# An edge-gated graph layer on one core: the gated halves made on GpSimd, the add done in place a tile ahead, z made in the rows of h

## The chip, the cores and the metric

The kernel runs on one core of a Trainium2 chip. The metric is the device time of one execution in microseconds. Engines are named as in the profile: PE is TensorE's matmuls, PEld its weight loads, DVE is VectorE, ACT is ScalarE, POOL is GpSimd, SP is SyncE, which here only issues DMAs. Every engine runs its own instructions strictly in the order in which they were written down.

## The reference

There are 16 graphs (`b`) with 1024 nodes and 256 features and one adjacency matrix for all, 1024 x 1024 with few entries that aren't zero. It is given as `A_a` and as `A_m`:

```python
pre_u = jnp.einsum('bud,dk->buk', h_t, W1[:d])
pre_v = jnp.einsum('bvd,dk->bvk', h_t, W1[d:])
hidden = jax.nn.relu(pre_u[:, :, None, :] + pre_v[:, None, :, :] + b1)
S = jax.nn.sigmoid(jnp.einsum('buvk,ko->buvo', hidden, W2)[..., 0] + b2[0])
a_t = jnp.einsum('buv,bud->bvd', S * A_a, h_t)
m_t = jnp.einsum('uv,bud->bvd', A_m, h_t) * h_t
z_t = beta1 * h_t + beta2 * (jnp.einsum('bvd,de->bve', a_t, Wa) + ba) + beta3 * (jnp.einsum('bvd,de->bve', m_t, Wm) + bm)
```

Each node `v` collects its neighbours' rows twice: weighted with the adjacency value (`m`), and with that value times a gate per edge and graph (`a`).

## The kernel before, in words

**Tiling.** Graphs go in four groups of `GB` = 4, nodes `v` in eight tiles of 128. A block is one group and one node tile; there are `BS` = 32 blocks, in the order of `order`. The edges of a node tile are sorted into two halves of 64 nodes (`w`), and each half into `TW` = 5 tiles of 128 edges (`j`). So a block has ten steps `s`, and the program has 320 steps `n`.

**Before the steps** the kernel makes neighbour lists from the adjacency (`lists`, for four of the node tiles up front and for the other four between the steps), and tables in DRAM, one for each group, whose row for a node holds `pre_u` of four graphs and `h` of four graphs: 8 KB. `rows` makes the `pre_u` part on PE (`w_u`, L427) with a copy on ACT (L443) and a store on SP (L446). Tables 1 to 3 are filled between the steps; the calls of `plan` give the steps of each load and of its two pieces.

**A step** `n` has these parts, each a function:

- `fetch` (L496): an indirect DMA on POOL fetches one row of the table for each of the 128 edges into `fetched[n % NF]`, `NF` = 6 places. The fetch for step n+5 is issued in step n, behind the aggregation of n-1, whose place it takes. `fetch_val` (L382) fetches adjacency values in the same queue, two in a step while there are any (80 in all, ten of them ahead of the steps).
- `expand` (L569): two matmuls on PE spread `pre_v + b1` of the 64 nodes to their edges, into the PSUM tile `pc`, of which there are two. It is called for n+2 near the end of step n.
- `left_adj` (L579): ACT writes the adjacency value, one-hot over 16 nodes, into the half of `left` that isn't gated, four times over, once for each graph. `left` has one slot of nodes (64 elements for both kinds and four graphs of 16 nodes: one quarter) or two, by `QUARTERS`: in the five tiles 1, 2, 2, 2, 1.
- `gate` (L601, L606, L609, L612): VectorE adds the fetched `pre_u` and `pc` into the one tile `t` (L601, 128 x 1024); four times, once for each graph, it takes the relu, multiplies by `W2` and sums (L606, with a read of the accumulator); ACT makes the sigmoid (L609) and then writes the gated half of `left` in four operations (L612). `fill` puts a list operation in front of each L606 while lists are made.
- `aggregate` (L623), called for n-1 in step n, ahead of the gate of n: matmuls of `left` with the fetched `h`, 8 or 16 matmul records, into `acc`.

**The end of a block** runs in the next block's steps. `half_end` copies `acc` (L631); `turn_over` transposes it (L641, steps 1, 7, 7, 9) and ACT copies it into `LT` (L644); VectorE multiplies the ungated half by `h` (L654). `block_end` (steps 3 to 6) multiplies with `Wa` and `Wm` (L672) in two halves; ACT copies each half out of PSUM into `z` (L675), VectorE adds `beta1 * h` two steps later (L676), and SP stores `z` (L678). `h` itself is the tile `h_blk`, loaded by SP in step 0 (L775). `halves` (steps 0, 2, 3, 5, 6) makes the next block's `pre_v`: `w_v` on PE (L427, behind a row of bias, L431), ACT copies (L461, L462, L465, L468) and a subtraction on VectorE (L463). All these PSUM tiles, `misc`, come from two banks of `psm`.

**What orders the work.** The order is written out by hand (`manual_schedule`): the order of the calls in the loop from L745 on is the order of each engine's queue. `after(step, f)` puts `f` down for a later step, and `do(step)` runs what is due, behind the gate of that step. SP runs as far ahead as its waits allow.

Of the kernel before, what the change touches and what calls it, by code (L numbers as in the profile page):

```python
# [13 lines left out]
P = 128  # L14
# [3 lines left out]
def kernel(  # L18
# [210 lines left out]
    NF = 6  # L229
# [327 lines left out]

    marks, pcs, accs, evs, hbs, LTs, lefts = {}, {}, {}, {}, {}, {}, {}
# [38 lines left out]

    def gate(n):
        k, g, vt, w, j = where(n)
        t = one.tile([P, GB, D], FP, name="t")  # L600
        nc.vector.tensor_tensor(t, fetched[n % NF][:, :GD].rearrange("p (b d) -> p b d", b=GB),  # L601
                                pcs.pop(n).rearrange("p (b d) -> p b d", b=GB), ALU.add)
# [5 lines left out]
        gt = wk.tile([P, GB], FP, name="gt")  # L608
        nc.scalar.activation(gt, sc, AF.Sigmoid, bias=b2_b)  # L609
        for b in range(GB):  # L610
            m = len(QUARTERS[j])
            nc.scalar.activation(lefts[n][:, :m, b, 1, :], lefts[n][:, :m, b, 0, :], AF.Copy, scale=gt[:, b:b + 1])  # L612

    def aggregate(n):
        k, g, vt, w, j = where(n)
        left, f = lefts.pop(n), fetched[n % NF]
        for i, q in enumerate(QUARTERS[j]):
# [4 lines left out]
            for b in range(GB):  # L622
                nc.tensor.matmul(accs[h][b * 2 * V:(b + 1) * 2 * V, r, :],  # L623
                                 left[:, i, b].rearrange("p k v -> p (k v)"), f[:, GD + b * D:GD + (b + 1) * D],
                                 start=first, stop=(j == q + 1), skip_group_check=True)
# [7 lines left out]
    def turn_over(k, w, q, step):  # L633
        if w == 0 and q == 0:
            LTs[k] = one.tile([P, DC, GB, 2, P], FP, name="LT")
        LT = LTs[k]
        pt = small("pt")
        ev = evs.pop(q)
        for i in range(4):
            r, c = divmod(i, DC)  # L640
            nc.tensor.transpose(pt[:, i * P:(i + 1) * P], ev[:, r, c * P:(c + 1) * P], ident)  # L641
        v = slice(w * W + q * U, w * W + (q + 1) * U)
        r = (w * W + q * U) // V
        nc.scalar.copy(LT.rearrange("p c b k (r v) -> p r (c b k) v", v=V)[:, r:r + 2],  # L644
                       pt.rearrange("p (r i v) -> p r i v", r=2, v=V))
# [6 lines left out]
        def times_h():  # L652
            m = LT[:, :, :, 0, v]
            nc.vector.tensor_tensor(m, m, hTs[order[k]].rearrange("p b c n -> p c b n")[:, :, :, v], ALU.mult)  # L654
# [4 lines left out]
    def block_end(k):  # L659
# [3 lines left out]
        z = big.tile([P, GB, D], FP, name="z", bufs=1)  # L663
        for h in range(2):
            for i, wt in ((1, w_a), (0, w_m)):
# [4 lines left out]
                for bb in range(2):  # L670
                    for c in range(DC):
                        nc.tensor.matmul(pz[:, bb * D:(bb + 1) * D], LTs[k][:, c, 2 * h + bb, i, :], wt[:, c, :],  # L672
                                         start=False, stop=(i == 0 and c == DC - 1), skip_group_check=True)
# [18 lines left out]
    def tail(parts, step):  # L692
# [8 lines left out]
        for i, wt in enumerate((w_m, w_a)):  # L701
            for r in range(len(parts)):
                for d in range(DC):
                    for b in range(c):
                        bb = r * c + b
                        nc.tensor.matmul(pz[b * m:(b + 1) * m, r * D:(r + 1) * D], LT[:, d, bb, i, v:v + m],  # L706
# [19 lines left out]
    def plan(blocks, ns):  # L726

        for k, (load, *pieces) in zip(blocks, ns):
# [7 lines left out]
                                                                             for i in range(2, NT - 1)), (223, 231, 233)))  # L736
# [7 lines left out]
    total = BS * T  # L744
    for n in range(total + 2):  # L745
        k, s = divmod(n, T)
        if 1 <= n <= total:
# [13 lines left out]
        if n + 2 < total:  # L761
            expand(n + 2)
# [181 lines left out]
```

## Time and profile before

| what | value |
|---|---|
| median of 3 runs | 1150.17 us (1149.06 to 1153.97) |
| the profiled execution, first to last instruction | 1165.8 us; the profile gives no time around it |
| busy | PE 94%, DVE 91%, ACT 77%, POOL 38% |
| granted TensorE clock | 0.976 on average, 1.00 from 310 us on |
| DMA | 391.40 MB, mean 336 GB/s |

The profile gives busy time by engine, groups of instructions by line with their mean duration and the idle time ahead of them, and timelines with the start of every instruction in us from the start of the span. Two things help in reading it. A duration on DVE, ACT and PE has a tail in which the next instruction already runs, so what an instruction costs in a full queue is the distance between two starts. And the waiting of an engine is put down to whatever came last, which in a queue can be the instruction ahead of the one that had to wait.

### The profile page before, as it was taken

The numbers are of one execution on the slowest core, as the hardware profiler recorded it, in microseconds if no ns is written. First come the engines' busy times: TensorE is split into PE (matmuls) and PEld (weight loads), VectorE is DVE, ScalarE is ACT, GpSimd is POOL, SyncE is SP. The second block draws the span as 40 slices with busy tenths as digits, with TensorE's granted clock in tenths as the row PEclk, the third lists the DMA queues.
The fourth block names the chain that finished last, engine by engine and source line by source line (L and its number), as shares of the span: only waits on it lengthen the run. The fifth ranks groups of instructions, "written<-read, shape, count | busy, mean of one in ns | idle before, by whom it ended". The sixth has DMA issues, their size and how long they took to land. (4 is left out here: it accounts for less than half of the span.)

```text
span 1165.8 us, 23918 instructions
## 1 busy us (share of the span) xinstructions
PE 1092.1 (94%) x7633; PEld 723.1 (62%) x7633; DVE 1056.2 (91%) x3487; ACT 893.5 (77%) x2624; POOL 439.9 (38%) x428
## 2 busy tenths in 40 slices
PE   7867899999999999999999999999999999999986
PEld 6744666666666666666666666666666666666553
DVE  7688889888999989999999999999999999999994
ACT  2346587767887878888888888888888888888873
POOL 1556645253335333443333333333333333333330
PEclk9868899999999999999999999999999999999999
DMA  9986898999999999999999999999998998999991
GB/s 286 298 307 223 277 372 312 362 320 331 342 320 323 396 379 336 358 350 402 389 374 369 355 364 356 360 364 383 371 375 324 361 322 333 334 339 328 328 346 60
DMA packets 147048, 391.40 MB, mean 336 GB/s; under 512 B 16753, under 2 KB 105329, under 8 KB 110705
## 3 DMA queue, kind: packets, MB, share of 16 engines
q0 software_dynamic: 50016, 300.50, 68.9%
q1 hardware_dynamic: 81616, 74.99, 20.0%
q10 hardware_dynamic: 15280, 14.29, 3.7%
q8 instruction: 63, 1.03, 0.3%
q14 instruction: 73, 0.59, 0.1%
HBM read 393.78 MB, written 50.33 MB: 381 GB/s over the span
## 5 line engine op out<-in xcount | busy, mean ns | idle before, releaser
L496 POOL DMA_INDIRECT fetched<-table,uidx x320 | 341.5, 1067 | 628.3 <-PE acc L623 447.2
L606 DVE SCALAR_TENSOR_TENSOR t<-t,w_b 128x256 f32<-128x256 f32 x1280 | 478.3, 421 | 19.3 <-ACT left L612 0.5
L601 DVE TENSOR_TENSOR t<-fetched,pc 128x1024 f32<-128x1024 f32 x320 | 389.3, 1217 | 41.4 <-PE pc L569 13.9
L623 PE MATMUL acc<-fetched,left 128*32 128x256 f32 x4096 | 336.2, 391 | 31.9 <-ACT left L612 26.2
L612 ACT ACTIVATE left<-left,gt 128x32 f32<-128x32 f32 (+1 forms) x1280 | 299.3, 304 | 10.4
L569 PE MATMUL pc<-X,mark 128*128 128x512 f32 x640 | 237.6, 453 | 6.2 <-ACT mark L562 5.0
L623 PEld LDWEIGHTS acc<-fetched,left 128*32 128x32 f32 x4096 | 130.6, 109 | 179.3 <-issue 52.4
L569 PEld LDWEIGHTS pc<-X,mark 128*128 128x128 f32 x640 | 97.2, 191 | 140.0 <-issue 89.3
L609 ACT ACTIVATE gt<-sc,b_b 128x4 f32<-128x4 f32 x320 | 96.2, 301 | 43.4 <-DVE t L606 40.8
L672 PE MATMUL misc<-w_m,LT 128*128 128x256 f32 x496 | 117.2, 379 | 0.0
L672 PE MATMUL misc<-w_a,LT 128*128 128x256 f32 x496 | 117.1, 379 | 0.0
L579 ACT ACTIVATE left<-onehot,val 128x128 f32<-128x128 bf16 (+1 forms) x320 | 116.5, 364 | 0.0
L427 PE MATMUL misc<-w_v,hT 128*128 128x256 f32 x448 | 107.3, 383 | 0.0
L427 PE MATMUL misc<-w_u,hT 128*128 128x256 f32 x416 | 101.2, 390 | 5.7 <-ACT few L329 3.6
L606 DVE DVE_READ_ACCUMULATOR t<-t,w_b 128x1 f32 x1280 | 104.0, 81 | 0.0
L672 PEld LDWEIGHTS misc<-w_a,LT 128*128 128x128 f32 x496 | 93.9, 189 | 15.1
L672 PEld LDWEIGHTS misc<-w_m,LT 128*128 128x128 f32 x496 | 93.8, 189 | 14.9
L382 POOL DMA_INDIRECT val<-in_adjT_dram,vidx x80 | 85.7, 1071 | 35.1 <-issue 22.4
L427 PEld LDWEIGHTS misc<-w_v,hT 128*128 128x128 f32 x448 | 86.0, 192 | 13.9
L427 PEld LDWEIGHTS misc<-w_u,hT 128*128 128x128 f32 x416 | 79.5, 195 | 17.3 <-ACT few L329 3.7
L631 ACT COPY ev<-acc 128x512 f32<-128x512 f32 x128 | 75.5, 590 | 14.6 <-PE acc L623 4.2
L675 ACT COPY z<-misc 128x512 f32<-128x512 f32 x62 | 36.3, 586 | 58.1 <-PE misc L672 38.8
(164 smaller groups left out, 947.9 us busy)
## 6 DMA issues: line engine op xcount, KB each, us to landing
h_blk<-in_x_dram SPq DMA_DIRECT2D x31, 512.0 KB
out_dram<-z SPq DMA_DIRECT2D x31, 512.0 KB
hT<-in_xT_dram SPq DMA_DIRECT2D x28, 512.0 KB
table<-in_x_dram ACTq DMA_DIRECT2D x24, 512.0 KB
table<-tab SPq DMA_DIRECT2D x24, 512.0 KB
fetched<-table,uidx POOLq DMA_INDIRECT x320
table<-in_x_dram SPq DMA_DIRECT2D x8, 512.0 KB
table<-fetched SPq DMA_DIRECT2D x8, 512.0 KB
```

The costliest lines, as they stand in the source:

```text
L382: nc.gpsimd.indirect_dma_start(out=val[:, i, j:j + 1], out_offset=None, in_=adj_flat, in_offset=bass.IndirectOffsetOnAxis(ap=vidx[:, i, j: ...
L427: nc.tensor.matmul(p[:, bb * D:(bb + 1) * D], hT[:, 2 * h + bb, i, :], wt[:, i, :], start=(i == 0 and not begun), stop=(i == DC - 1), skip ...
L496: nc.gpsimd.indirect_dma_start(out=fetched[n % NF], out_offset=None, in_=table[g], in_offset=bass.IndirectOffsetOnAxis(ap=uidx[:, vt * NW ...
L569: nc.tensor.matmul(pcs[n][:, c], marks[n // TW][:, j * P:(j + 1) * P], cuts[k][:, w, c], start=True, stop=True)
L579: nc.scalar.activation(lefts[n][:, :m, :, 0, :], onehot[:, i, o:o + m, :].unsqueeze(2).to_broadcast([P, m, GB, V]), AF.Copy, scale=val[:, ...
L601: nc.vector.tensor_tensor(t, fetched[n % NF][:, :GD].rearrange("p (b d) -> p b d", b=GB), pcs.pop(n).rearrange("p (b d) -> p b d", b=GB), ...
L606: nc.vector.scalar_tensor_tensor(t[:, b, :], t[:, b, :], 0.0, w2_b, ALU.max, ALU.mult, accum_out=sc[:, b:b + 1])
L609: nc.scalar.activation(gt, sc, AF.Sigmoid, bias=b2_b)
L612: nc.scalar.activation(lefts[n][:, :m, b, 1, :], lefts[n][:, :m, b, 0, :], AF.Copy, scale=gt[:, b:b + 1])
L623: nc.tensor.matmul(accs[h][b * 2 * V:(b + 1) * 2 * V, r, :], left[:, i, b].rearrange("p k v -> p (k v)"), f[:, GD + b * D:GD + (b + 1) * D ...
L631: nc.scalar.copy(evs[q], accs.pop(q))
L672: nc.tensor.matmul(pz[:, bb * D:(bb + 1) * D], LTs[k][:, c, 2 * h + bb, i, :], wt[:, c, :], start=False, stop=(i == 0 and c == DC - 1), sk ...
```

## The change

- `NF` goes from 6 to 7. The fetch for step n+6 is now issued in step n.
- The add is a function of its own, `add`, works in the fetched rows themselves and is called for n+1 in step n, ahead of the gate of n. `add(0)` stands in front of the loop.
- `gate` ends with the sigmoid. `weigh` makes the gated halves of all four graphs in one GpSimd operation, called for n-1 at the start of step n, ahead of the aggregation of n-1 and of the fetch that follows it.
- `left` has two gated slots around one ungated slot that both use, so `left_adj` writes half as much. `LT` is laid out to match: for every second graph the two kinds are swapped, and `turn_over`, `times_h`, `block_end` and `tail` index it so.
- `expand(n + 2)` moves from behind `do(n)` to the start of step n.
- `z` has no tile any more. L675 is gone; VectorE reads PSUM and writes into `h_blk`, one step after the matmuls rather than two, and `h_blk` is what is stored.
- The last table row's steps go from (223, 231, 233) to (222, 230, 232).

```diff
-    NF = 6
+    NF = 7
...
-        lefts[n] = wk.tile([P, 2, GB, 2, V], FP, name="left")
-        nc.scalar.activation(lefts[n][:, :m, :, 0, :], onehot[:, i, o:o + m, :].unsqueeze(2).to_broadcast([P, m, GB, V]),
+        lefts[n] = wk.tile([P, 2, 2 * GB, V], FP, name="left")
+        nc.scalar.activation(lefts[n][:, :m, 1::GB, :],
+                             onehot[:, i, o:o + m, :].unsqueeze(2).to_broadcast([P, m, GB // 2, V]),
                              AF.Copy, scale=val[:, i, j:j + 1])
...
+    def add(n):
+        ts[n] = t = fetched[n % NF][:, :GD]
+        nc.vector.tensor_tensor(t, t, pcs.pop(n), ALU.add)
+
     def gate(n):
-        k, g, vt, w, j = where(n)
-        t = one.tile([P, GB, D], FP, name="t")
-        nc.vector.tensor_tensor(t, fetched[n % NF][:, :GD].rearrange("p (b d) -> p b d", b=GB),
-                                pcs.pop(n).rearrange("p (b d) -> p b d", b=GB), ALU.add)
+        t = ts.pop(n).rearrange("p (b d) -> p b d", b=GB)
         sc = wk.tile([P, GB], FP, name="sc")
         for b in range(GB):
             fill(n)
             nc.vector.scalar_tensor_tensor(t[:, b, :], t[:, b, :], 0.0, w2_b,
                                            ALU.max, ALU.mult, accum_out=sc[:, b:b + 1])
-        gt = wk.tile([P, GB], FP, name="gt")
-        nc.scalar.activation(gt, sc, AF.Sigmoid, bias=b2_b)
-        for b in range(GB):
-            m = len(QUARTERS[j])
-            nc.scalar.activation(lefts[n][:, :m, b, 1, :], lefts[n][:, :m, b, 0, :], AF.Copy, scale=gt[:, b:b + 1])
+        gates[n] = wk.tile([P, 1, GB, 1], FP, name="gt")
+        nc.scalar.activation(gates[n].rearrange("p i b j -> p (i b j)"), sc, AF.Sigmoid, bias=b2_b)
+
+    def weigh(n):
+        m = len(QUARTERS[n % TW])
+        left = lefts[n]
+        nc.gpsimd.tensor_tensor(left[:, :m, ::2, :], left[:, :m, 1:2, :].to_broadcast([P, m, GB, V]),
+                                gates.pop(n).to_broadcast([P, m, GB, V]), ALU.mult)
...
-            LTs[k] = one.tile([P, DC, GB, 2, P], FP, name="LT")
+            LTs[k] = one.tile([P, GB, 2, DC, P], FP, name="LT")
...
-            nc.scalar.copy(z[:, sl], pz.rearrange("p (b d) -> p b d", b=2))
-            after(step + 2, lambda sl=sl: nc.vector.scalar_tensor_tensor(z[:, sl], hb[:, sl], be1, z[:, sl],
-                                                                         ALU.mult, ALU.add))
+            after(step + 1, lambda sl=sl, pz=pz: nc.vector.scalar_tensor_tensor(
+                hb[:, sl], hb[:, sl], be1, pz.rearrange("p (b d) -> p b d", b=2), ALU.mult, ALU.add))
         after(step + 3, lambda: nc.sync.dma_start(
-            out[g * GB:(g + 1) * GB, vt * P:(vt + 1) * P, :].rearrange("b p d -> p b d"), z))
+            out[g * GB:(g + 1) * GB, vt * P:(vt + 1) * P, :].rearrange("b p d -> p b d"), hb))
...
-                                                                             for i in range(2, NT - 1)), (223, 231, 233)))
+                                                                             for i in range(2, NT - 1)), (222, 230, 232)))
...
+    add(0)
     for n in range(total + 2):
         k, s = divmod(n, T)
+        if n + 2 < total:
+            expand(n + 2)
+        if 1 <= n <= total:
+            weigh(n - 1)
+        if n + 1 < total:
+            add(n + 1)
         if 1 <= n <= total:
             aggregate(n - 1)
             fetch_val(2)
...
-        if n + 2 < total:
-            expand(n + 2)
```

More of the change, by code (lines that the diff above doesn't have):

```diff
@@ L553, in scale_late @@
         nc.vector.tensor_scalar(w_m, w_m, be3, None, ALU.mult)
+    ts, gates = {}, {}
     marks, pcs, accs, evs, hbs, LTs, lefts = {}, {}, {}, {}, {}, {}, {}
@@ L623, in aggregate @@
                 nc.tensor.matmul(accs[h][b * 2 * V:(b + 1) * 2 * V, r, :],
-                                 left[:, i, b].rearrange("p k v -> p (k v)"), f[:, GD + b * D:GD + (b + 1) * D],
+                                 left[:, i, 2 * b - b % 2:2 * b - b % 2 + 2].rearrange("p k v -> p (k v)"), f[:, GD + b * D:GD + (b + 1) * D],
                                  start=first, stop=(j == q + 1), skip_group_check=True)
@@ L634, in turn_over @@
         if w == 0 and q == 0:
-            LTs[k] = one.tile([P, DC, GB, 2, P], FP, name="LT")
+            LTs[k] = one.tile([P, GB, 2, DC, P], FP, name="LT")
         LT = LTs[k]
-        pt = small("pt")
+        pt = small("pt").rearrange("p (r k c v) -> p r k c v", r=2, c=DC, v=V)
         ev = evs.pop(q)
@@ L640, in turn_over @@
             r, c = divmod(i, DC)
-            nc.tensor.transpose(pt[:, i * P:(i + 1) * P], ev[:, r, c * P:(c + 1) * P], ident)
+            nc.tensor.transpose(pt[:, r, :, c, :], ev[:, r, c * P:(c + 1) * P], ident)
         v = slice(w * W + q * U, w * W + (q + 1) * U)
         r = (w * W + q * U) // V
-        nc.scalar.copy(LT.rearrange("p c b k (r v) -> p r (c b k) v", v=V)[:, r:r + 2],
-                       pt.rearrange("p (r i v) -> p r i v", r=2, v=V))
+        nc.scalar.copy(LT.rearrange("p b k c (r v) -> p r (b k c) v", v=V)[:, r:r + 2],
+                       pt.rearrange("p r k c v -> p r (k c) v"))
         apart = k == BS - 1 and w == NW - 1
@@ L652, in times_h @@
         def times_h():
-            m = LT[:, :, :, 0, v]
-            nc.vector.tensor_tensor(m, m, hTs[order[k]].rearrange("p b c n -> p c b n")[:, :, :, v], ALU.mult)
+            m = LT.rearrange("p (b two) k c n -> p b (two k c) n", two=2)[:, :, DC:3 * DC, v]
+            h = hTs[order[k]].rearrange("p (b two) c n -> p b (two c) n", two=2)[:, :, :, v]
+            nc.vector.tensor_tensor(m, m, h, ALU.mult)
             if w == NW - 1 and q == 1:
@@ L662, in block_end @@
         hb = hbs[k]
-        z = big.tile([P, GB, D], FP, name="z", bufs=1)
         for h in range(2):
@@ L671, in block_end @@
                     for c in range(DC):
[L672 removed]
+                        nc.tensor.matmul(pz[:, bb * D:(bb + 1) * D], LTs[k][:, 2 * h + bb, i if bb else 1 - i, c, :], wt[:, c, :],
                                          start=False, stop=(i == 0 and c == DC - 1), skip_group_check=True)
             sl = slice(2 * h, 2 * h + 2)
[L675 to L677 removed]
+            after(step + 1, lambda sl=sl, pz=pz: nc.vector.scalar_tensor_tensor(
+                hb[:, sl], hb[:, sl], be1, pz.rearrange("p (b d) -> p b d", b=2), ALU.mult, ALU.add))
         after(step + 3, lambda: nc.sync.dma_start(
[L679 removed]
+            out[g * GB:(g + 1) * GB, vt * P:(vt + 1) * P, :].rearrange("b p d -> p b d"), hb))
         del hbs[k], LTs[k]
@@ L705, in tail @@
                         bb = r * c + b
-                        nc.tensor.matmul(pz[b * m:(b + 1) * m, r * D:(r + 1) * D], LT[:, d, bb, i, v:v + m],
+                        nc.tensor.matmul(pz[b * m:(b + 1) * m, r * D:(r + 1) * D], LT[:, bb, i if bb % 2 else 1 - i, d, v:v + m],
                                          wt[:, d, :], start=False, stop=(i == 1 and d == DC - 1), skip_group_check=True)
```

## The prediction, on record before the result

> **What bounds the kernel now.** I read the page's busy times and groups first, then four stretches of the span, and inside these the timeline of each engine. No engine leads on the page:
>
> ```profile
> PE 1092.1 (94%) x7633; PEld 723.1 (62%) x7633; DVE 1056.2 (91%) x3487; ACT 893.5 (77%) x2624; POOL 439.9 (38%) x428
> L496 POOL DMA_INDIRECT fetched<-table,uidx x320 | 341.5, 1067 | 628.3 <-PE acc L623 447.2
> L606 DVE SCALAR_TENSOR_TENSOR t<-t,w_b 128x256 f32<-128x256 f32 x1280 | 478.3, 421 | 19.3 <-ACT left L612 0.5
> L601 DVE TENSOR_TENSOR t<-fetched,pc 128x1024 f32<-128x1024 f32 x320 | 389.3, 1217 | 41.4 <-PE pc L569 13.9
> L612 ACT ACTIVATE left<-left,gt 128x32 f32<-128x32 f32 (+1 forms) x1280 | 299.3, 304 | 10.4
> ```
>
> The starts of the 320 adds of L601 cut the span into A (blocks 0 to 5, 39.6 us a block of ten steps), B (6 to 11, 34.0), C (12 to 23, 32.03), D (24 to 30, 31.3) and an end of 48 us. A and B still make neighbour lists; A to C make table rows (L427 `w_u`); D makes neither.
>
> ```profile
> 72.00:310.00 238.00, 216.90 (x1428) 143.80 (x1427) 205.92 (x707) 169.04 (x495) 117.00 (x113) 0.94 0.89 311
> 310.00:513.00 203.00, 196.20 (x1394) 130.01 (x1394) 193.21 (x648) 164.11 (x483) 85.71 (x81) 1.00 0.96 352
> 513.00:897.00 384.00, 382.27 (x2766) 252.18 (x2764) 362.83 (x1144) 324.99 (x969) 130.35 (x122) 1.00 0.99 368
> 897.00:1117.00 220.00, 212.48 (x1531) 134.79 (x1529) 211.08 (x666) 185.69 (x560) 73.68 (x71) 1.00 0.92 335
> ```
>
> Columns: stretch, length, then PE, PEld, DVE, ACT, POOL busy, granted clock, DMA share, GB/s. In C TensorE is busy 382 of 384 us at the full clock. To see whether that is work or waiting I read the starts in one block of C:
>
> ```profile
> 801.35 1.07 PE L623 MATMUL acc<-fetched,left 128*32 128x256 f32 x16
> 802.35 0.73 PE L569 MATMUL pc<-X,mark 128*128 128x512 f32 x2
> 802.92 0.60 PE L641 MATMUL misc<-ident,ev 128*128 128x128 f32 x4
> 803.45 0.64 PE L623 MATMUL acc<-fetched,left 128*32 128x256 f32 x8
> ...
> 826.80 1.07 PE L623 MATMUL acc<-fetched,left 128*32 128x256 f32 x16
> 827.80 0.73 PE L569 MATMUL pc<-X,mark 128*128 128x512 f32 x2
> 828.37 1.03 PE L641 MATMUL misc<-ident,ev 128*128 128x128 f32 x8
> 829.34 1.65 PE L623 MATMUL acc<-fetched,left 128*32 128x256 f32 x16
> ```
>
> Nothing idles between them. From one tile's aggregation to the next this block has 2.10, 3.18, 3.39, 3.63, 3.62, 3.38, 3.20, 2.95, 2.54 and 3.39 us: 31.4 us of plain TensorE work, against 32.03 on average. So C is bound by TensorE, and D, with two `w_u` groups of 1.82 us fewer (27.7 us), is not: there VectorE is busy 211 of 220 us.
>
> **VectorE: the gain.** Start to start is what counts.
>
> ```profile
> 1000.40 0.08 DVE L606 DVE_READ_ACCUMULATOR t<-t,w_b 128x1 f32 x1
> 1000.57 1.22 DVE L601 TENSOR_TENSOR t<-fetched,pc 128x1024 f32<-128x1024 f32 x1
> 1001.89 0.42 DVE L606 SCALAR_TENSOR_TENSOR t<-t,w_b 128x256 f32<-128x256 f32 x1
> ```
>
> The add starts 0.17 us after the last accumulator read, since it overwrites the one `t`; the first L606 starts late because it reads the add's result (median 1.25 us after the add's start; 1.14 where an independent list operation follows instead). In place and a tile ahead, both waits go: 10 x 0.11 + 5 x 0.17 (in half the steps another operation stands between) = 2.0 us a block. A block of VectorE work becomes 10 x (1.14 + 4 x 0.346) + 2 x 0.665 (L676) + 2 x 0.604 (L654) + 1.14 (L463) = 28.9 us, from 31.3. L676 now reads PSUM; L601, which reads PSUM, and L463, which does not, both take 1.22 us for 1024 elements, so I price that at nothing. VectorE then stops being the bound anywhere but in the list steps of B, where a list operation already covers the 0.11.
>
> **ScalarE** loses 299 us of L612 and 36 us of L675; L579 writes half as much. This pays only where TensorE waits for `left`: 15.1 (weight loads) and 10.4 us (matmuls), partly the same waits, in A. I take -10 us there.
>
> **GpSimd: the new loop.** Its queue holds, per step: halves of tile n-1, fetch into the place of tile n-1, halves of tile n. The fetch waits until the aggregation of n-1 has read its place, and the halves of n stand behind it, and the aggregation of n behind those. Today the fetch blocks nobody. So from the last matmul of one aggregation to the first of the next there is a handover H:
>
> - last L623 start to fetch start: 0.53 us (median over 300 to 1,100 us);
> - the fetch: 0.99;
> - a gap after it: 0 to 0.30, seen between two issues:
>
> ```profile
> 178.05 1.00 POOL L382 DMA_INDIRECT val<-in_adjT_dram,vidx  x1 [0.30 <-issue]
> 179.35 1.00 POOL L382 DMA_INDIRECT val<-in_adjT_dram,vidx  x1 [0.30 <-issue]
> ```
>
> - the multiply of 64 or 128 elements, which no row shows: from 0.16 (GpSimd memset of 80 elements) to 0.55 (its plain DMA issue), and I take 0.32, by its one reduction (0.316);
> - semaphore to TensorE: 0.05 to 0.16, by ScalarE's end of L612 to the weight load that waited.
>
> H is 1.73 to 2.53; the middle values give 2.1, and I take 2.2 because the multiply shares the stretch with busy engines. An aggregation's own starts span 0.69 us (16 matmuls) or 0.26 (8), so no two aggregations can start nearer than H + 0.69 or H + 0.26. At 2.2 the 2.10 of step 9 becomes 2.89 and the 2.54 of step 7 becomes 2.89: C has 31.4 + 1.1 = 32.5 us a block, +6 us over its twelve. In D also the steps that lost `w_u` (1.57 us) become 2.46 and 2.89: 27.7 + 1.1 + 0.9 + 1.3 = 31.1, -2 us over seven.
>
> Of the 80 fetches of `val`, 70 stand in this queue in 35 steps, two ahead of the fetch; three issues of 1.30 and a multiply make 4.2 us a step, where A has 3.96 and some have 3.8. Cost: 35 x 0.3 = +10 us, which eats ScalarE's -10.
>
> The GPSIMD Engine Reference of the Trainium skill (§ 3.1) gives 2.6 cycles an element for two inputs: by it the multiply of 128 elements is an estimated 0.28 us plus dispatch, and H hardly differs.
>
> L606 reads both inputs from SBUF for 478 us, and no GpSimd row here reads two tiles beside it. The Trainium skill, SBUF — State Buffer (§ Who interferes with whom), says that such an instruction contends with a GpSimd one that reads SBUF, the second to issue blocking: that speaks against this change, and if each multiply lost one L606 of 0.35 us, H would be 2.55 and C alone would be 14 us longer than today.
>
> **The rest.** Seven places: the fetch goes one step further ahead, but the add is also one step earlier, and the lead stays five steps; fetches land 7 to 9 us after issue and up to 7 us before their add, but nearly late (0.1) in C. DMA is at 0.99 there, so nothing is to be won by faster engines. One table row is made a step earlier, since table 3 must be written ahead of its first fetch; that fetch waited 3.8 us before 889 us, and now halves wait behind it: +3 us once. Out of `h_blk`: its load waits for the store to land (3 to 11 us) and SP's `xT` load stands behind it; both have eight steps (25 us), less one step gained by the earlier L676: nothing, or some 2 us a block of C if late. Expansion first moves two matmuls ahead of the aggregation that they already followed: nothing. L676 holds its PSUM bank until VectorE reads it; VectorE is ahead of TensorE by then: nothing. Lists of B: -4 us.
>
> **Sum.** A 0, B -4, C +6, D -2, table +3: +3 us on the profiled execution, whose span of 1165.8 us is the time I have for it, with nothing around it shown, and which is 1.4% above the median of 1150.17. Scaled by 0.987 this is 1153.
>
> **Rivals.** *Short handover* (H 1.73): C has one step late by 0.3 us, -4; D falls to 29.3, -14; B -5; A -8 by ScalarE: -31, so 1120. For it: the multiply is small, and VectorE's 2 us are certain. *Long handover* (H 2.53): C 33.2, +14; D 32.4, +8; A +5 by the `val` fetches: +27, so 1177. It decides from about H = 2.3, at the GpSimd queue of L496, and its light steps 7 and 9 pay first. For it: the fetch's wait stands in front of the multiply in every step. *Late rows of h*: the store's landing pushes `h_blk` past its step in the twelve blocks of C: 12 x 2 on top of the sum, so 1177; DMA at 0.99 speaks for it, 8 steps of lead against. *No gain in VectorE* (the add still waits after the reads, on another event): D back to 31.3 and B without its 4, so 1159, inside the forecast's own case.
>
> **Chances.** The forecast's own case (H 2.1 to 2.35), 1144 to 1162: 0.40, of which 0.24 within 0.5% (about what a measurement here can tell from no change) and 0.16 slower. Short handover, 1120 to 1144: 0.33, faster. Long handover, 1162 to 1190: 0.20. Late rows: 0.07. Faster 0.33, same 0.24, slower 0.43. The range 1128 to 1180 leaves about a tenth at each side.
>
> **What will tell.** Right: L601's successor 1.14 us behind it; VectorE below 93% busy in D; GpSimd's multiply near 0.3 us directly behind each fetch; weight loads of L623 waiting for GpSimd in steps 7 and 9 (and 1 and 8 in D). Wrong: a multiply above 0.6 us, L606 stretched beyond 421 ns, L676 waiting for `h_blk`, or blocks of D under 30 us.

## The result, and the profile after

The changed kernel takes **1203.15 us** (median of 4, 1198.25 to 1204.44); the kernel before took 1149.62 us beside it (1147.13 to 1153.97). The ratio is **1.045**, with a 95% interval of 1.042 to 1.049: slower, and outside the predicted range. Between the two profiled executions the span goes from 1165.8 to 1202.4 us, by 36.6.

One thing must be known before numbers are compared. Beside the experiments the kernel before takes 1169 us and the changed one 1207, a ratio of 1.032 (1.028 to 1.036). So some 16 us of the first difference belong to executions of the kernel before at 1150 us. Both its profiles have a span of 1166 us, so nothing here shows where those 16 to 20 us go: that stays open. Everything below compares profiles with each other, or times with those of the kernel before that were taken beside them.

The page of the changed kernel, busy times and groups:

```profile
PE 1049.6 (87%) x7633; PEld 689.4 (57%) x7633; DVE 1091.1 (91%) x3487; ACT 558.8 (46%) x1282; POOL 580.1 (48%) x748
L496 POOL DMA_INDIRECT fetched<-table,uidx x320 | 341.3, 1067 | 500.5 <-PE acc L629 382.7
L609 DVE SCALAR_TENSOR_TENSOR fetched<-fetched,w_b 128x256 f32<-128x256 f32 x1280 | 536.6, 464 | 0.0
L602 DVE TENSOR_TENSOR fetched<-fetched,pc 128x1024 f32<-128x1024 f32 x320 | 387.5, 1211 | 68.7 <-PE pc L570 68.2
L629 PE MATMUL acc<-fetched,left 128*32 128x256 f32 x4096 | 290.4, 390 | 113.0 <-POOL left L617 112.4
L617 POOL TENSOR_TENSOR left<-left,gt 128x128 f32<-128x128 f32 (+1 forms) x320 | 141.2, 441 | 35.8 <-ACT gt L612 18.4
```

ScalarE went from 894 to 559 us, as priced. The sum of L609 went from 421 to 464 ns, and the aggregation (L629) now waits 112 us for GpSimd's multiply (L617). The four stretches, cut as before (length, then PE, PEld, DVE, ACT, POOL busy, granted clock, DMA share, GB/s):

```profile
72.00:310.00 238.00, 203.76 (x1407) 134.24 (x1405) 206.21 (x696) 106.66 (x243) 142.53 (x170) 0.94 0.89 311
310.00:518.00 208.00, 189.19 (x1404) 124.27 (x1406) 196.09 (x651) 103.53 (x237) 113.42 (x141) 1.00 0.96 350
518.00:932.00 414.00, 377.21 (x2784) 246.57 (x2776) 384.79 (x1144) 200.38 (x467) 180.93 (x241) 0.98 0.95 343
932.00:1152.00 220.00, 196.54 (x1519) 123.18 (x1512) 220.00 (x666) 110.02 (x260) 105.22 (x140) 1.00 0.92 329
```

A and D take what they took; B takes 5 us more by these cuts, C 30. By the starts of the adds, which cut more exactly, in us:

| kernel | span | A | B | C | block 12 (part of C) | D | D, median block | end |
|---|---|---|---|---|---|---|---|---|
| before | 1165.8 | 237.8 | 203.8 | 384.4 | 32.2 | 219.9 | 31.3 | 48.3 |
| changed | 1202.4 | 237.8 | 207.8 | 413.8 | 52.6 | 220.0 | 31.4 | 50.7 |

**Two thirds of what C lost are in one block.** GpSimd there:

```profile
524.85 0.31 POOL L617 TENSOR_TENSOR left<-left,gt 128x64 f32<-128x64 f32 x1
526.15 1.22 POOL L496 DMA_INDIRECT fetched<-table,uidx  x1 [1.00 <-PE acc L629]
536.28 0.40 POOL L838 PARTITION_ALL_REDUCE longest<-rest  x1 [8.91 <-issue]
543.50 0.28 POOL L617 TENSOR_TENSOR left<-left,gt 128x64 f32<-128x64 f32 x1 [6.82 <-issue]
```

This is the program's only `partition_all_reduce`, the maximum over the partitions that closes the neighbour lists. It runs for 0.40 us, but 8.91 us pass ahead of it and 6.82 us between it and the next multiply, and neither is put down to another engine ("issue"). Each gap begins with two instructions MODIFY_POOL_CONFIG: of the reduction's line at 527.4 us, right behind the fetch, and of the multiply's line at 536.6 us. A first such pair of the multiply's line stands at 75.2 us, ahead of the program's first multiply (76.40), and costs nothing like it. The kernel before has one pair, ahead of its reduction, but its GpSimd does no arithmetic between the steps, and there the reduction starts at once:

```profile
518.31 0.99 POOL L496 DMA_INDIRECT fetched<-table,uidx  x1 [0.30 <-issue]
519.51 0.32 POOL L828 PARTITION_ALL_REDUCE longest<-rest  x1 [0.21 <-issue]
```

TensorE of the changed kernel stands behind the multiply for 15.37 us:

```profile
527.65 0.81 PE L570 MATMUL pc<-X,mark 128*128 128x512 f32 x2
543.84 1.08 PE L629 MATMUL acc<-fetched,left 128*32 128x256 f32 x8 [15.37 <-POOL left L617]
```

and its granted clock (the number ahead of the last two, which are DMA share and GB/s) falls while it waits, and stays down for the first 6 us of the work that follows:

```profile
529.00:532.80 3.80, 0.00 (x0) 0.00 (x0) 2.10 (x9) 1.16 (x4) 0.00 (x0) 1.00 0.99 404
532.80:549.90 17.10, 6.06 (x22) 4.15 (x22) 0.00 (x0) 1.07 (x2) 2.34 (x4) 0.50 0.19 63
549.90:556.00 6.10, 6.10 (x50) 3.99 (x50) 5.81 (x16) 3.18 (x9) 2.69 (x3) 1.00 0.85 246
```

**The rest is the handover that was forecast.** The timeline of one light step, with the instructions between left out:

```profile
700.85 1.07 PE L629 MATMUL acc<-fetched,left 128*32 128x256 f32 x16 [0.50 <-POOL left L617]
...
701.36 0.07 DVE L609 DVE_READ_ACCUMULATOR fetched<-fetched,w_b 128x1 f32 x1
701.36 1.21 DVE L602 TENSOR_TENSOR fetched<-fetched,pc 128x1024 f32<-128x1024 f32 x1
...
702.22 1.03 POOL L496 DMA_INDIRECT fetched<-table,uidx  x1 [1.43 <-PE acc L629]
...
702.49 0.41 DVE L609 SCALAR_TENSOR_TENSOR fetched<-fetched,w_b 128x256 f32<-128x256 f32 x1
702.84 0.08 DVE L609 DVE_READ_ACCUMULATOR fetched<-fetched,w_b 128x1 f32 x1
702.84 0.60 DVE L609 SCALAR_TENSOR_TENSOR fetched<-fetched,w_b 128x256 f32<-128x256 f32 x1
703.29 0.41 POOL L617 TENSOR_TENSOR left<-left,gt 128x128 f32<-128x128 f32 x1
703.38 0.07 DVE L609 DVE_READ_ACCUMULATOR fetched<-fetched,w_b 128x1 f32 x1
703.38 0.61 DVE L609 SCALAR_TENSOR_TENSOR fetched<-fetched,w_b 128x256 f32<-128x256 f32 x1
703.75 0.59 PEld L629 LDWEIGHTS acc<-fetched,left 128*32 128x32 f32 x16 [1.60 <-POOL left L617]
703.75 1.07 PE L629 MATMUL acc<-fetched,left 128*32 128x256 f32 x16 [1.17 <-POOL left L617]
```

Three things are to be seen. The fetch of 702.22 waits for the aggregation of 700.85; the multiply waits behind the fetch; the next aggregation, at 703.75, waits for the multiply: 2.90 us from aggregation to aggregation, though TensorE had little else to do. VectorE's gain is there: the add starts with the last read (701.36), and its successor 1.13 us behind it. And two of the L609 that a multiply overlaps take 0.60 us rather than 0.41, which is the contention that was weighed.

So there are three suspects, for D above all: the handover, the contention, and no gain in VectorE. D's 31.4 us is about what the rival "no gain in VectorE" gave (31.3), and VectorE is busy for all 220.00 of its 220 us, as if it were the bound. The experiments show that neither the second reading nor the third holds.

### The profile page after: what moved, and what is told of

It reads as the page before. It is cut to its first block, busy times and chain, and to the rows that moved or that the text cites. A ratio compares the mean times of both kernels' runs of the same rounds, so it can differ in the third digit from the quotient of the medians.

```text
span 1202.4 us, 23583 instructions
## 1 busy us (share of the span) xinstructions
PE 1049.6 (87%) x7633; PEld 689.4 (57%) x7633; DVE 1091.1 (91%) x3487; ACT 558.8 (46%) x1282; POOL 580.1 (48%) x748
## 3 DMA queue, kind: packets, MB, share of 16 engines
q8 instruction: 63, 1.03, 0.3%
## 4 chain that ended last, share of the span: by engine, by line
DVE 29%; PE 22%; issue 15%; DMA 7%; POOL 6%; ACT 1%; POOLq 0%; ACTq 0%; DVEq 0%
DVE fetched L609 15%; DVE fetched L602 10%; PE misc L427 6%; PE acc L629 6%; DMA fetched<-table,uidx 4%; PE misc L678 4%; POOL fetched L496 3%; PE pc L570 3%; POOL left L617 2%; DMA val<-in_adjT_dram,vidx 2%; PE misc L431 2%; DVE low L463 1%; DVE LT L661 1%; DMA key<-in_adjT_dram 1%; PE misc L647 1%
## 5 line engine op out<-in xcount | busy, mean ns | idle before, releaser
L609 DVE SCALAR_TENSOR_TENSOR fetched<-fetched,w_b 128x256 f32<-128x256 f32 x1280 | 536.6, 464 | 0.0
L602 DVE TENSOR_TENSOR fetched<-fetched,pc 128x1024 f32<-128x1024 f32 x320 | 387.5, 1211 | 68.7 <-PE pc L570 68.2
L629 PE MATMUL acc<-fetched,left 128*32 128x256 f32 x4096 | 290.4, 390 | 113.0 <-POOL left L617 112.4
L570 PE MATMUL pc<-X,mark 128*128 128x512 f32 x640 | 253.3, 477 | 5.4 <-ACT mark L563 5.0
L629 PEld LDWEIGHTS acc<-fetched,left 128*32 128x32 f32 x4096 | 100.8, 109 | 271.8 <-POOL left L617 168.3
L617 POOL TENSOR_TENSOR left<-left,gt 128x128 f32<-128x128 f32 (+1 forms) x320 | 141.2, 441 | 35.8 <-ACT gt L612 18.4
L612 ACT ACTIVATE gt<-sc,b_b 128x4 f32<-128x4 f32 x320 | 95.8, 299 | 127.3 <-DVE fetched L609 126.8
L570 PEld LDWEIGHTS pc<-X,mark 128*128 128x128 f32 x640 | 115.2, 192 | 25.5 <-ACT mark L563 5.0
L650 ACT COPY LT<-misc 128x512 f32<-128x512 f32 x128 | 72.1, 587 | 75.7 <-PE misc L647 75.7
L580 ACT ACTIVATE left<-onehot,val 128x64 f32<-128x64 bf16 (+1 forms) x320 | 103.7, 324 | 0.1
L609 DVE DVE_READ_ACCUMULATOR fetched<-fetched,w_b 128x1 f32 x1280 | 98.3, 77 | 0.0
```

The costliest lines, as they stand in the source:

```text
L570: nc.tensor.matmul(pcs[n][:, c], marks[n // TW][:, j * P:(j + 1) * P], cuts[k][:, w, c], start=True, stop=True)
L580: nc.scalar.activation(lefts[n][:, :m, 1::GB, :], onehot[:, i, o:o + m, :].unsqueeze(2).to_broadcast([P, m, GB // 2, V]), AF.Copy, scale=v ...
L602: nc.vector.tensor_tensor(t, t, pcs.pop(n), ALU.add)
L609: nc.vector.scalar_tensor_tensor(t[:, b, :], t[:, b, :], 0.0, w2_b, ALU.max, ALU.mult, accum_out=sc[:, b:b + 1])
L612: nc.scalar.activation(gates[n].rearrange("p i b j -> p (i b j)"), sc, AF.Sigmoid, bias=b2_b)
L617: nc.gpsimd.tensor_tensor(left[:, :m, ::2, :], left[:, :m, 1:2, :].to_broadcast([P, m, GB, V]), gates.pop(n).to_broadcast([P, m, GB, V]), ...
```

## The experiments

The times are medians, with the kernel before on the same chip: 1169.39 us (e1 to e4), 1169.70 (e5 to e8), 1168.91 (e9 to e12). C and D are those stretches of the profiled execution, in us.

| run | us | ratio, 95% | C | D |
|---|---|---|---|---|
| e1_before_again | 1168.4 | one run | 384.5 | 220.1 |
| e5_after_again | 1207.2 | 1.032 (1.028 to 1.036) | 411.3 | 220.0 |
| e2_no_reduce | 1189.5 | 1.017 (1.015 to 1.019) | 396.8 | 220.0 |
| e9_fetch_behind_gate | 1152.7 | 0.985 (0.981 to 0.988) | 383.5 | 205.1 |
| e4_fetch_later | 1158.9 | 0.990 (0.986 to 0.993) | 383.5 | 217.8 |
| e11_halves_on_gpsimd_alone | 1192.5 | 1.020 (1.017 to 1.023) | 395.8 | 225.7 |
| e6_halves_write_only | 1193.2 | 1.021 (1.017 to 1.025) | 394.3 | 218.8 |
| e10_halves_twice | 1307.9 | 1.118 (1.115 to 1.121) | 434.1 | 262.8 |
| e3_halves_on_act | 1146.0 | 0.982 (0.978 to 0.987) | 384.0 | 204.8 |
| e7_act_six_places | 1157.4 | 0.988 (0.983 to 0.993) | 384.7 | 212.6 |
| e8_act_six_two_h | 1156.8 | 0.988 (0.984 to 0.993) | 384.2 | 208.8 |
| e12_quarter_of_the_store | 1140.0 | one run | 378.7 | 204.9 |

### How far two executions agree: e1, e5

Both kernels unchanged.

> The kernel before, unchanged, for a second profile: the first one's span (1165.8 us) was 1.4% above its timed runs, that of the changed kernel (1202.4) was not. Expected: a span of about 1148 us, with blocks of 31.3 to 31.7 us in stretches C and D; the 16 us that go missing then show in which stretch the first profile hid part of the loss. If the span is again 1165, the profile itself lengthens the kernel before and not the changed one.

> The changed kernel, unchanged, in the same call as the next three. In the call of e1 to e4 the kernel before took 1169 us and not 1150, so the loss has to be measured again beside it. Expected from e2 (1189.5) and the 15.7 us of idle GpSimd time around its reduction: 1205 to 1210 us.

The second profile of the kernel before has the span of the first (1166.3 and 1165.8 us), and the executions timed beside it take 1169 us too, so nothing speaks for a profile that lengthens it. Its A to D come again within 0.7 us each. Those of the changed one differ by 3.1 (A), 2.4 (B) and 2.5 us (C, all of it in block 12: 52.6 and 50.1, with gaps of 7.54 and 7.19 us around the reduction), and D is the same. So a stretch tells of nothing below some 3 us in A to C.

### The reduction: e2

On the changed kernel; the same maximum is taken with a transpose on TensorE, a reduction on VectorE, a matmul (`across`, which lays the eight maxima into one row) and a second reduction:

```diff
-            nc.gpsimd.partition_all_reduce(longest, rest, P, bass_isa.ReduceOp.max)
-            after(n + 12, count_rest)
+            pl = small("pl")
+            nc.tensor.transpose(pl[:NT, :P], rest, ident)
+            after(n + 1, lambda pl=pl: nc.vector.tensor_reduce(longest[:NT, 0:1], pl[:NT, :P], AX.X, ALU.max))
+            after(n + 3, across)
```

> The changed kernel, with the one GpSimd reduction over partitions (step 120) made by a transpose on TensorE and a maximum on VectorE instead. Theory: around that reduction GpSimd loads code twice (8.9 and 6.8 us of idle time), and since the gated halves stand in its queue everything waits; without it 16 to 20 us go, 1203 becomes 1183 to 1187, and block 12 takes 33 us instead of 52.6. Rival (the long step comes from late data or from TensorE): block 12 stays above 45 us and the time at 1200.

Each against the kernel before on its chip, the difference falls from +37.5 (e5) to +20.1 us: **the reduction costs 17.4 us**, once, for 0.40 us of work. Block 12 goes from 50.1 to 34.5 us, which is 15.6 of them. That it is not the reduction itself is seen in two profiles: with no multiply around it, it waits 0.21 us (the kernel before, and e3), and its two MODIFY_POOL_CONFIG are there too. With multiplies around it the gap comes on both sides, so it is the change from one operation to the other that costs. The first of the two kinds that a program runs had no such gap: the reduction in the kernel before, the multiply in the changed one. That code is loaded in the gaps is inferred, since no row shows a load. The experiments below that keep the multiply on GpSimd start from e2, so that this is out of the way.

### The handover: e9, e4

On e2. e9 keeps every instruction and turns GpSimd's queue round: the halves of tile n stand ahead of the fetches that wait for the aggregation of n-1.

```diff
-        if 1 <= n <= total:
-            weigh(n - 1)
...
             aggregate(n - 1)
-            fetch_val(2)
-            if n - 1 + NF < total:
-                fetch(n - 1 + NF)
...
             gate(n)
+            weigh(n)
             if n + 1 < total:
                 left_adj(n + 1)
+        if 1 <= n <= total:
+            fetch_val(2)
+            if n - 1 + NF < total:
+                fetch(n - 1 + NF)
```

> As e2, with GpSimd's queue turned round: the halves of tile n stand right behind the gate of n and ahead of the fetch for the place of n-1, so that no halves wait for an aggregation and the fetch keeps its lead of five steps (e4 gave one up). Handover theory: D at 29.0 to 29.5 us a block, C at 384, 1145 to 1155 us, some 35 us under e2 and at or under e4 (1159). If instead the halves now delay the fetches (they wait for VectorE's gate), VectorE waits for rows and it stays above 1165.

The queue then looks like this, in a step of D with TensorE's aggregations around it:

```profile
953.98 1.07 PE L634 MATMUL acc<-fetched,left 128*32 128x256 f32 x16
954.28 0.40 POOL L622 TENSOR_TENSOR left<-left,gt 128x128 f32<-128x128 f32 x1 [0.69 <-ACT gt L617]
955.35 1.03 POOL L496 DMA_INDIRECT fetched<-table,uidx  x1 [0.68 <-PE acc L634]
956.47 1.07 PE L634 MATMUL acc<-fetched,left 128*32 128x256 f32 x16
```

The multiply (954.28) waits for its gate alone, and the fetch, which waits for the aggregation of 953.98, comes behind it. From aggregation to aggregation it is 2.49 us; the same step takes 3.06 in e2.

From +20.1 to -16.2 us: **the order in the queue costs 36.3 us**, and without it, and without the reduction, the change is faster than the kernel before. By stretch, e2 to e9: A -3, B -4, C -13, D -15 (the two spans differ by 32.4 us; start and end took 2.7 more). D's block falls to 29.0 us, VectorE's own 28.9, and VectorE is busy in 198 of 200 us. Most of the stretching is gone as well (L614, the former L609, has a mean of 425 ns), since the multiply now runs beside VectorE's add; so e9 alone doesn't tell the handover from the contention, and e6 below does:

```profile
900.00:1100.00 200.00, 191.44 (x1469) 120.83 (x1468) 198.21 (x648) 109.39 (x254) 101.87 (x138) 1.00 0.95 354
```

e4 leaves the order and takes the wait away, with a fetch into the place of tile n-2, which has long been read:

```diff
-            if n - 1 + NF < total:
-                fetch(n - 1 + NF)
+            if n >= 2 and n - 2 + NF < total:
+                fetch(n - 2 + NF)
```

> As e2, and the fetch that GpSimd issues behind the halves of tile n-1 is the one for the place of tile n-2, already read, so that no halves wait behind an unfinished aggregation; the fetch lead falls from five steps to four. Handover theory (fetch wait plus issue in front of the halves sets the light steps): steps 7 and 9 return to about 2.6 and 2.2 us between aggregations, C to 31.6 us a block and D to 30.5 or less, some 12 to 18 us below e2, unless fetches then come late. Contention theory (VectorE, busy all the time in D because the GpSimd multiply takes its second input, sets the pace): within 4 us of e2.

-10.5 us against the kernel before, so 30.7 from e2. Most blocks of D take 29.1 us here too; two take 36 us, in which VectorE (L686, the former L681) waits 6.7 and 7.1 us for `h_blk` to be loaded. Two quite different edits with one thing in common, that no multiply stands behind a waiting fetch, give back the same 2.3 to 2.4 us a block.

### GpSimd's part alone: e11

On the kernel before, with the reduction as in e2: only the four L612 become one GpSimd multiply, ahead of the fetch of its step.

```diff
-        for b in range(GB):
-            m = len(QUARTERS[j])
-            nc.scalar.activation(lefts[n][:, :m, b, 1, :], lefts[n][:, :m, b, 0, :], AF.Copy, scale=gt[:, b:b + 1])
+    def weigh(n):
+        m = len(QUARTERS[n % TW])
+        left = lefts[n]
+        nc.gpsimd.tensor_tensor(left[:, :m, :, 1, :], left[:, :m, :, 0, :],
+                                gates.pop(n).to_broadcast([P, m, GB, V]), ALU.mult)
```

> The kernel before with one part of the change alone: the gated halves made by GpSimd ahead of the fetch (and its reduction made on TensorE and VectorE, as in e2); the add, z, the places and the expansion stay as before. Handover theory: C as e2, 33 us a block, +12. In D the handover allows 31.4 as in e2, but VectorE had no slack there (31.3), so each multiply that takes L606's second input (0.2 us of stretch in about half of the tiles and more) now shows: 32.5 to 34 us a block, +8 to +18. In all 1195 to 1215 us, against 1169 before and 1189 for e2: the part costs more alone than beside the add ahead. If it is under 1180, the loss needs the other parts.

+23.6 us, against +20.1 for everything together (e2). With the halves on GpSimd, the add in place, the seven places and `z` in `h_blk` bring 3.5 us; e3 shows that they are worth 23 without it. The time is 2.5 us under the range that was expected, and most blocks of D take 31.8 us, not 32.5 or more: what the stretching costs without slack in VectorE was put too high.

### Contention or handover: e6, e10

e6, on e2: GpSimd only writes, in about as much busy time (103.6 us in D, 105.7 in e2).

```diff
-        left = lefts[n]
-        nc.gpsimd.tensor_tensor(left[:, :m, ::2, :], left[:, :m, 1:2, :].to_broadcast([P, m, GB, V]),
-                                gates.pop(n).to_broadcast([P, m, GB, V]), ALU.mult)
+        gates.pop(n)
+        for _ in range(2):
+            nc.gpsimd.memset(lefts[n][:, :m, ::2, :], 0.5)
```

> As e2, but GpSimd's multiply is two memsets of the same places (the gates are left out: the gated half is the constant 0.5), so that its operation writes SBUF for about as long and reads nothing. Contention theory (the multiply reads SBUF and so holds up L606's successor, which reads two tiles from it; VectorE then sets the pace in D): the mean duration of that line falls from 464 to 421 ns, its starts from 0.41 back to 0.346 us apart, and D falls from 31.4 to below 30 us a block, the whole by 12 us or more under e2. Handover theory (fetch in front of the halves sets the pace, VectorE is merely stretched into its slack): the line shrinks as well, VectorE then waits for TensorE, and the time falls by no more than the memsets are shorter, 0 to 6 us.

Its page and its D:

```profile
L614 DVE SCALAR_TENSOR_TENSOR fetched<-fetched,w_b 128x256 f32<-128x256 f32 x1280 | 476.1, 422 | 0.0
```

```profile
932.00:1152.00 220.00, 196.79 (x1505) 122.26 (x1505) 205.69 (x675) 108.99 (x257) 103.64 (x211) 0.99 0.93 330
```

The stretching is gone (464 to 422 ns; from start to start 0.413 to 0.345 us, which over 1280 sums and 320 multiplies is 0.27 us for each multiply), and VectorE is busy 205.7 rather than 220.0 us of D. The time is not less: +23.5 us against e2's +20.1. A block of D still takes 31.3 us, against 31.4. **The contention is real and costs next to nothing here**: it only filled the time in which VectorE would have waited for the handover. An engine that is busy all the time need not be the bound, since instructions that are held up count as busy. The rule of the Trainium skill that the prediction weighed, SBUF — State Buffer (§ Who interferes with whom), agrees in kind, also in that an operation that only writes doesn't disturb.

e10, on e2: the multiply done twice, to lengthen the handover.

```diff
-        left = lefts[n]
-        nc.gpsimd.tensor_tensor(left[:, :m, ::2, :], left[:, :m, 1:2, :].to_broadcast([P, m, GB, V]),
-                                gates.pop(n).to_broadcast([P, m, GB, V]), ALU.mult)
+        left, gt = lefts[n], gates.pop(n)
+        for _ in range(2):
+            nc.gpsimd.tensor_tensor(left[:, :m, ::2, :], left[:, :m, 1:2, :].to_broadcast([P, m, GB, V]),
+                                    gt.to_broadcast([P, m, GB, V]), ALU.mult)
```

> As e2, with GpSimd's multiply done twice into the same places. The handover grows by one multiply, 0.36 to 0.57 us. By the slack that the changed kernel's trace shows between the end of the multiply and the aggregation (0.05 us in steps 7 and 9 and, in D, in 1 and 8; 0.40 in step 8 of C; 0.46 or more in all others) D grows by 4 x 0.45, to 33.2 us a block, and C by about 0.45 + 0.35 + 0.1, to 33.6 apart from its odd blocks: +12 and +11 us, with A and B some +25 to +35 us, 1215 to 1225. If VectorE's stretched instructions set the pace, it grows in all ten steps alike: the multiply overlaps them for twice as long, some 2.5 us a block, +75 us.

+139 us against the kernel before, 119 more than e2: several times what was expected. A block of D takes 37.5 us rather than 31.4. TensorE in one of these blocks:

```profile
993.44 1.07 PE L635 MATMUL acc<-fetched,left 128*32 128x256 f32 x16 [1.04 <-POOL left L623]
994.44 0.73 PE L575 MATMUL pc<-X,mark 128*128 128x512 f32 x2
997.51 1.07 PE L635 MATMUL acc<-fetched,left 128*32 128x256 f32 x16 [2.34 <-POOL left L623]
...
1002.28 3.54 PE L427 MATMUL misc<-w_v,hT__6557 128*128 128x256 f32 x8
```

Eight matmuls of `w_v` take 3.54 us here, and 1.89 elsewhere in the block. The granted clock shows why:

```profile
992.00:998.80 6.80, 3.41 (x39) 1.42 (x38) 6.80 (x22) 2.10 (x7) 3.83 (x6) 1.00 0.90 284
998.80:1005.60 6.80, 6.40 (x24) 4.15 (x22) 3.62 (x15) 1.61 (x4) 3.27 (x6) 0.50 0.97 382
```

TensorE was busy for half of the first stretch and is given half the clock in the next. This comes once in each block of D, every 37.5 us. The 6.1 us that a block lost can be taken apart by the starts of the aggregations (medians over D, e2 and e10). 2.4 us are in one step, the one with half the clock (3.19 and 5.55 us). 3.7 us are in steps 1, 2, 3, 7, 8 and 9, by 0.3 to 1.2 us each. Steps 4 and 5 take 3.39 and 3.19 us in both. So the loss does not come in all ten steps alike, as it would if VectorE's stretched instructions set the pace, and e10 supports the handover. As a measure of its length it failed: it grew by twice the 1.8 us that were expected. Two multiplies take 1.13 and 1.40 us ahead of the first two aggregations shown, not twice 0.41, and the price of the clock was in neither sum.

### The change without GpSimd: e3, and what else it holds: e7, e8

e3, on the changed kernel: the halves stay on ScalarE, all else is kept.

```diff
-    def weigh(n):
...
+        for b in range(GB):
+            nc.scalar.activation(lefts[n][:, :m, 2 * b, :], lefts[n][:, :m, 1, :], AF.Copy, scale=gt[:, b:b + 1])
```

> The changed kernel with only the GpSimd part undone: the four gated halves are made by ScalarE right behind the sigmoid, as before the change; all the rest of the change stays. Theory (the loss is in GpSimd's queue and its port, the VectorE part is a gain): L606's successor falls back to 421 ns mean, blocks of C take 31.4 to 31.8 us and blocks of D 28.9 to 30 us, 1120 to 1137 us in all, faster than the kernel before. Rival (the loss is in the other edits: h_blk stored and reloaded, z read from PSUM, expansion first): above 1165 us.

**Faster than both kernels**: 1146.0 us, 0.982 (0.978 to 0.987) of the kernel before, so by some 2%. In the spans, against e1: A -4, B -6, C 0, D -15. A block of D takes 29.3 us; the prediction had 28.9 for VectorE. The whole gain of the change is here.

e7 is e3 with `NF = 6`, e8 is e7 with two tiles for the rows of `h`:

```diff
-    NF = 7
+    NF = 6
...
-            hbs[k - 1] = big.tile([P, GB, D], FP, name="h_blk", bufs=1)
+            hbs[k - 1] = big.tile([P, GB, D], FP, name="h_blk", bufs=2)
```

> As e3, with six places for fetched rows instead of seven; with the add a tile ahead the fetch lead falls from five steps to four. If the seventh place is what lets the add go ahead, VectorE waits for fetches (8 to 10 us to land against four steps of 3.1 us, less TensorE's lag): C over 33 us a block, 1160 us or more. If the lead is ample, as e4's blocks of 29.1 us in D suggest: 1146 us as e3, within 6 us.

> As e7, with two tiles for the rows of h (the space of the place that e7 gives up), so that their load and the xT load behind it in SP's queue no longer wait for the store to land. Theory (the store in front of the loads makes the late rows: 7 us in block 13 of e3): no block of C stands out above 34 us but block 23, 5 to 10 us under e7, 1136 to 1142 us. Rival (the late rows come from the crowded DMA queues alone): as e7 within 4 us, with late blocks still there.

By the medians the seventh place is worth 11 us (1157.4 against 1146.0), between the two values that were expected; the intervals of the two ratios overlap, so the time alone doesn't settle it. The profiles do: D takes 212.6 us rather than 204.8, and the add waits 33.7 us for the rows of its own fetch, which takes 0.6 us in e3. The page of e7:

```profile
L602 DVE TENSOR_TENSOR fetched<-fetched,pc 128x1024 f32<-128x1024 f32 x320 | 390.2, 1220 | 85.8 <-DMA fetched<-table,uidx 33.7
```

The second tile for `h` brings nothing that can be told (1156.8 and 1157.4): the late rows of `h` delay single blocks and were not a bound. It is a weak test, since e7 has no block as late as block 13 of e3 (39.0 us; the latest in C but block 23 is 34.5). In the trace of the changed kernel itself VectorE never waits for `h_blk` to be loaded.

### What bounds C: e12

e12 is e3 with a quarter of each store of the result:

```diff
-            out[g * GB:(g + 1) * GB, vt * P:(vt + 1) * P, :].rearrange("b p d -> p b d"), hb))
+            out[g * GB:g * GB + 1, vt * P:(vt + 1) * P, :].rearrange("b p d -> p b d"), hb[:, 0:1]))
```

> As e3, but only one of a block's four graphs is stored (three quarters of the results of all blocks but the last are left out): 384 KB less of some 11.7 MB a block to move. C took 383.5 to 384.7 us in six kernels with quite different engines' loads, at a DMA share of 0.99 to 1.00. If the DMA engines set it, C falls by 2 to 3%, to 373 to 378 us (TensorE's own work, 31.4 us a block, ends at 377). If TensorE sets it, C stays at 382 to 385.

The span falls by 4.1 us, and C by 5.3, to 378.7, which is neither of the two ranges. It comes from one block: block 13, 39.0 us in e3, takes 31.3, while block 23 takes 2.4 more. In e3 TensorE waits there for a transposed `h` that comes late, and pays with its clock too:

```profile
545.35 3.78 PE L427 MATMUL misc<-w_v,hT 128*128 128x256 f32 x8 [4.78 <-DMA hT<-in_xT_dram]
```

Six of C's twelve blocks take 31.2 to 31.3 us in e12 and in e3 alike, which is TensorE's own work (31.4 by the prediction). In one stretch of them, 540 to 575 us in e12, TensorE is busy all 35.0 us at the full clock. So C's regular blocks are TensorE's, at a DMA share over C of 0.97 (e12) as at 0.99 (e3), and the full DMA only makes the odd block late. With that, C comes to 383.5 to 384.7 us in seven executions (the kernel before, e1, e3, e4, e7, e8, e9): what the change frees on VectorE and ScalarE finds nothing to shorten there.

## Why the prediction was wrong

The forecast said 1153 us, the result 1203. Three errors make up most of the 50 us: 20 for what GpSimd does around its reduction, 8 in B, 15 by the scale. By the terms of the sum:

| term | predicted | measured, profile to profile |
|---|---|---|
| A | 0 | 0.0 |
| B | -4 | +4.0 |
| C without block 12, table 3 included | +8.5 (11/12 of 6, and 3) | +9.0 |
| block 12 | +0.5 | +20.4 |
| D | -2 | +0.1 |
| start and end | 0 | +3.0 |
| sum | +3 | +36.6 |
| scaling by 0.987 | -15 | not seen |

**1. The step that failed: GpSimd's new loop was priced as a queue alone.** The prediction listed what stands in GpSimd's queue in every step and what each instruction takes. It had no term for what else GpSimd does in the program, and took the one reduction only as a yardstick for the multiply (0.316 us). That yardstick came from a kernel in which nothing else ran in its place. Two changes of operation, with gaps of 8.91 and 6.82 us and TensorE's half clock behind them, made block 12 20 us longer (17 between the second profiles). The Trainium skill, GPSIMD Engine Reference (§ 2.1 Instruction dispatch), says that the first call to freshly loaded code pays some 6 us, with no instruction to be seen. The two gaps are longer, the second is ahead of an operation that had run 120 times before, and whether they are of that kind no row shows. No row of the trace of before could give the price. But the reduction's row and its two MODIFY_POOL_CONFIG were there, and nothing was kept in the range for what happens to them when GpSimd also multiplies.

**2. The `val` fetches were charged to A only.** They were priced at 35 steps of three issues and a multiply, 0.3 us each. But ten of these steps are in B, in blocks 7 and 11. GpSimd in block 7 of the changed kernel:

```profile
360.34 1.03 POOL L382 DMA_INDIRECT val<-in_adjT_dram,vidx  x1 [0.16 <-issue]
361.67 1.02 POOL L382 DMA_INDIRECT val<-in_adjT_dram,vidx  x1 [0.30 <-issue]
362.99 1.18 POOL L496 DMA_INDIRECT fetched<-table,uidx  x1 [0.30 <-ACT X L465]
364.20 0.41 POOL L617 TENSOR_TENSOR left<-left,gt 128x128 f32<-128x128 f32 x1
364.77 1.03 POOL L382 DMA_INDIRECT val<-in_adjT_dram,vidx  x1 [0.17 <-issue]
```

4.43 us from one to the next, with the queue full: the 4.2 of the prediction was nearly right, its place was not. A step of A had 3.96 us before, by the prediction; the ten steps of block 7 took 32.4 us in all, so there a step of 4.43 costs more than 0.3. Blocks 7 and 11 lost 3.3 and 3.6 us, to 35.7 and 35.9; they take 35.7 and 36.0 in e9 too, and 32.0 and 33.1 in e3, so it is the multiply and the issues in one queue, in whatever order. The gain of the list blocks came as forecast (blocks 6, 9 and 10: -4.3 us, for -4), and block 8 lost 1.4 to the handover (33.0 us; 31.0 in e9). In A the forecast of nothing held; its two halves, -10 and +10, were not measured apart.

**3. The scale.** +3 us on an execution of 1165.8 were taken down to 1153 by the median of the runs shown. The changed kernel has no such difference between profile and median (1202.4 and 1203.15). What makes the kernel before shorter in its runs at 1150 is in no profile; it was not to be assumed for the changed kernel.

**What held.** The mechanism and its size: H was forecast at 2.2 us and measures 2.17 to 2.37 in the light steps. Its parts, measured and (predicted): 0.68 (0.53) to the fetch, 1.03 (0.99), a gap of 0.03 (0.15), the multiply 0.38 to 0.59 (0.32), 0.05 to TensorE (0.05 to 0.16). The aggregations of an ordinary block of C stand 32.6 us apart over ten steps (32.5), of D 31.4 (31.1, and 0.3 seven times is the 2 us missed). Steps 7 and 9 pay in C, and in D steps 1 and 8 as well, as said. VectorE's gain was right (28.9, and 29.0 to 29.3 in e9 and e3). The contention was left out of the sum, and it costs next to nothing (e6). So the rival *long handover*, which had the sign, was wrong in H (2.53 us), *late rows of h* was not at work (VectorE doesn't wait for `h_blk` in the changed kernel's trace), and *no gain in VectorE* had D's number for the wrong reason.

**What the sum hid.** Set against the kernel before, the handover looked cheap. In D the forecast's own numbers hold a gain of 17 us (seven blocks from 31.3 to 28.9) and a loss of 15 (back to 31.1), and only the difference of 2 was written down. Measured against the same kernel without it, the handover costs 36 us (e9), more than twice the 16 us by which that kernel is faster than the one before.

## What to carry to other kernels

Before work is given to an engine, list everything that it runs over the whole program, not only in the loop: on GpSimd a second kind of operation can cost far more than it takes to run (here 17.4 us for 0.40), and everything that stands behind it waits as well. On an engine that runs in order, put an instruction that waits long behind those that someone waits for: here the same instructions in another order differ by 36 us. And a busy share of 100% is no proof of a bound while another engine stretches the instructions; only taking the disturbance away (e6) tells.

## What the runs showed of the hardware that was not expected

- **GpSimd's change of operation**: 8.91 us ahead of one `partition_all_reduce` and 6.82 us behind it when `tensor_tensor` runs on both sides (7.54 and 7.19 in e5); 0.21 us ahead of it when only DMA issues do. The first `tensor_tensor` of the program had no such gap.
- **The clock fell with TensorE half busy.** In e10 TensorE is busy 3.41 of 6.80 us, its longest wait in them being 2.34 us, and is then given 0.50 of its clock for 6.8 us; eight matmuls go from 1.89 to 3.54 us. In the changed kernel the low stretch was 17.1 us. A wait of TensorE cost twice there, which a sum of waits doesn't hold. The clock records of all 14 traces change only in steps of 3.41 us. Cut into these steps, from 120 us on and up to 8 us before the end, the traces have 4214 at the full clock. 47 of them were followed by half the clock: in 43 of these TensorE was busy for at most 45.7% of the step (37% in e10 from 995.38 to 998.79 us), in four for 60 to 75%, which stays open. In the other 4167 it was busy for at least 45.6%.
- **VectorE beside GpSimd's multiply**: a two-input sum of 256 elements goes from 0.35 us to 0.54 us from start to start while the multiply runs (702.84 to 703.38 us above), and stays at 0.345 beside writes alone. Over the program that is 0.27 us lost for each multiply of 0.44 us, and much less in e9 (a mean of 425 rather than 464 ns), where the multiply runs beside the add.
